# Zero products ahead of the first load, earlier routing loads and three copies on ScalarE in an attention and mixture-of-experts kernel

## The chip, the cores and the metric

The kernel runs on one core of a Trainium2 chip. The core has TensorE (matrix products, PE in the profile, with its weight loads as PEld), VectorE (DVE), ScalarE (ACT), GpSimd (POOL) and SyncE (SP), each with its own in-order queue of instructions; they meet at semaphores. DMA transfers are issued from such a queue (here mostly SP's). The metric is the device time of one execution in microseconds, as the median of several runs. A profile is one further execution that the hardware profiler took down.

## The reference

One sequence of S = 4096 rows with D = 256 columns, all in fp32, goes through one pre-norm block:

```python
x = x + attn(layernorm(x), Qw, Kw, Vw)          # causal, one head of 256
h = layernorm(x) @ W_in + b_in
logits = h @ W_gate + b_gate                    # 8 experts
topv, topi = top_k(softmax(logits), 2); topv /= sum(topv)
eout_e = relu(h @ W1[e] + b1[e]) @ W2[e] + b2[e]   # 256 -> 1024 -> 256
x = x + (sum over the two chosen e of topv * eout_e) @ W_out + b_out
```

## The kernel before, in words

The rows are held in SBUF in 8 blocks `xb[b]` of 512 rows (4 tiles of 128). The kernel has three stages.

*Attention, with the routing inside.* The weights of the queries and keys are folded into one: `prepare_scores` turns Qw and Kw with TensorE transposes into PSUM (L381, tiles pqwT and pkwT), ScalarE copies them out (L382), and TensorE multiplies them to pqk (L386), which VectorE scales into `qk_sb` (L393). For each block, `stats0` takes the layer norm's statistics on VectorE (L211, L212) with the reciprocal root on GpSimd (L217, L218); `ln_rows` makes the normalised rows z on VectorE (L231); `turn` transposes them (pz, L242) and VectorE copies them out as zT (L243); `project` makes the queries (pq, L406; copied as qT on VectorE, L413) and the values (pv, L418; copied on ScalarE, L425). `scores(g)` multiplies the scores of 256 queries with all keys up to them (ps, L448), adds the mask on the diagonal (L467), finds the row maxima (top, L473 to L478), turns them over with TensorE (pt, L484; pmax, L491), subtracts and takes the exponential (L495 to L504). `attend(g)` multiplies with the values (po, L513).

`prepare_biases` prepares the routing. It transposes a tile `brows`, which holds b1 (64 rows of 128) and b_in (2 rows), into pbias (L159); the copy biasT (L161) goes out to DRAM for the experts (L162). It transposes W_in, 128 columns at a time (pwin, L171), copies it out as winT (L172), multiplies it with W_gate (pwg, L176), and puts the product behind W_in's columns in `win_sb` (L183), so that one product later gives both h and the logits. b_in times W_gate (binc, L185; pbg, L190) is added to the gate's bias (L197). The transposes pbias and pwin take turns in two PSUM buffers (`ps_tr`), so the second half of pwin waits until biasT has been copied out of the first buffer.

*Experts.* Rows are scattered to the experts, taken in blocks of 256, halves and quarters; the weights of each come by DMA while TensorE works at the ones before (pm L743 and L773, pe L810). *The end.* The experts' results are read back, weighted, turned and multiplied with W_out (pa L997, pf L1011), added to x and stored.

What sets the order: each engine takes its instructions in the order of the built program. A scheduler decides that order from the order of the calls and from its own estimates, so instructions of `prepare_biases` stand among those of `scores(0)` and `scores(1)` on TensorE, and among the z of the second block on VectorE. `tc.issue_after` holds `stats0(1)` behind the projection of block 0. The loads at the front are issued from SP in the order of the calls (L119 to L136), with Kw and Qw ahead on ScalarE's queue (L107):

```python
for j in range(TPB):
    nc.sync.dma_start(out=xb[0][:, j, :], in_=xs[0][:, j, :])
vw_sb = load_square(Vw, "vw")
for b in range(1, NB):
    nc.sync.dma_start(out=xb[b], in_=xs[b])
```

After these come W_in, W_gate, W_out, the three bias rows and then brows.

Of the kernel before, what the change touches and what calls it, by code (L numbers as in the profile page):

```python
# [10 lines left out]
F32 = mybir.dt.float32  # L11
# [6 lines left out]
P = 128  # L18
# [3 lines left out]
QB = 256  # L22
# [12 lines left out]
def preln_attention_moe_kernel(  # L35
# [18 lines left out]
    nc = tc.nc  # L54

    _, S, D = x.shape
    NE, _, FF = W1.shape
    NT = S // P
    NB = S // TB
# [18 lines left out]
    xs = x.rearrange("o (b t p) d -> (o b) p t d", t=TPB, p=P)  # L78
    outs = out.rearrange("o (n p) d -> (o n) p d", p=P)

    const = ctx.enter_context(tc.tile_pool(name="const", bufs=1))
# [4 lines left out]
    def ps_mm(name):  # L86
        return psum.tile([P, TB], F32, tag="mm", name=name, bufs=4)

    def ps_tr(name):
        return psum.tile([P, TB], F32, tag="tr", name=name, bufs=2)  # L90

    def ps_o(name):
        return psum.tile([P, TB], F32, tag="o", name=name, bufs=2)
# [6 lines left out]
    parts = dram.tile([TOPK * S, D], F32, name="parts")  # L100


    xb = [stream.tile([P, TPB, D], F32, tag=f"x{b}", name=f"x{b}") for b in range(NB)]

    def load_square(w, name, queue=nc.sync):
        t = const.tile([P, ND, w.shape[1]], F32, tag=name, name=name)
        queue.dma_start(out=t, in_=w.rearrange("(c p) e -> p c e", p=P))  # L107
        return t

    def load_row(v, name):  # L110
        t = const.tile([P, v.shape[0]], F32, tag=name, name=name)
        nc.sync.dma_start(out=t, in_=v.partition_broadcast(P))
        return t
# [4 lines left out]
    for j in range(TPB):  # L118
        nc.sync.dma_start(out=xb[0][:, j, :], in_=xs[0][:, j, :])  # L119
    vw_sb = load_square(Vw, "vw")  # L120
    for b in range(1, NB):
        nc.sync.dma_start(out=xb[b], in_=xs[b])

    DG = D + NE
    win_sb = const.tile([P, ND, DG], F32, tag="win", name="win")
    nc.sync.dma_start(out=win_sb[:, :, :D], in_=W_in.rearrange("(c p) e -> p c e", p=P))
    wgate_sb = load_square(W_gate, "wgate")
    wout_sb = load_square(W_out, "wout")
    bgate_bc = load_row(b_gate, "bgate")
    bin_bc = load_row(b_in, "bin")  # L130
    bout_bc = load_row(b_out, "bout")

    NBR = NE * NF + ND
    brows = const.tile([NBR, P], F32, tag="brows", name="brows")
    nc.sync.dma_start(out=brows[: NE * NF, :], in_=b1.rearrange("e (f p) -> (e f) p", p=P))
    nc.sync.dma_start(out=brows[NE * NF :, :], in_=b_in.rearrange("(c p) -> c p", p=P))  # L136


    ident = const.tile([P, P], F32, tag="ident", name="ident")
# [5 lines left out]
        out=mask,  # L145
        in_=mask,
# [10 lines left out]
    def prepare_biases():  # L157
        ptb = ps_tr("pbias")
        nc.tensor.transpose(ptb[:, :NBR], brows, ident[:NBR, :NBR])  # L159
        biasT = const.tile([P, NBR], F32, tag="biasT", name="biasT")  # L160
        nc.vector.tensor_copy(biasT, ptb[:, :NBR])  # L161
        nc.sync.dma_start(  # L162
            out=bias1.rearrange("(e p) f -> p e f", p=P),
            in_=biasT[:, : NE * NF].rearrange("p (e f) -> p e f", f=NF),
        )

        winT = piece("winT", ND, D)
        for k in range(ND):
            pt = ps_tr(f"pwin{k}")
            for c in range(ND):  # L170
                nc.tensor.transpose(pt[:, ts(c, P)], win_sb[:, c, ts(k, P)], ident)  # L171
            nc.vector.tensor_copy(winT[:, k, :], pt[:, :D])  # L172
        for c in range(ND):
            pg = ps_o(f"pwg{c}")
            for k in range(ND):
                nc.tensor.matmul(  # L176
                    pg[:, :NE],
                    lhsT=winT[:, k, ts(c, P)],
                    rhs=wgate_sb[:, k, :],
                    start=(k == 0),  # L180
                    stop=(k == ND - 1),
                )
            nc.vector.tensor_copy(win_sb[:, c, D:], pg[:, :NE])  # L183
        binc = piece("binc", ND, P)
        nc.vector.tensor_copy(  # L185
            binc, biasT[:, NE * NF :].unsqueeze(2).to_broadcast([P, ND, P])
        )
        pg = ps_o("pbg")
        for k in range(ND):
            nc.tensor.matmul(  # L190
                pg[:, :NE],
                lhsT=binc[:, k, :],
                rhs=wgate_sb[:, k, :],
                start=(k == 0),
                stop=(k == ND - 1),
            )
        nc.vector.tensor_tensor(bgate_bc, pg[:, :NE], bgate_bc, ALU.add)  # L197
# [165 lines left out]
    def piece(name, *shape):  # L363

        return attn.tile([P, *shape], F32, tag="s", name=name, bufs=NS)
# [486 lines left out]
    for e in range(NE):  # L852
# [17 lines left out]
        out=rows[TOPK * (S - TB) :, :].rearrange("(t p) d -> p t d", p=P),  # L870
        in_=zero.unsqueeze(1).to_broadcast([P, TOPK * (TPB + 1), D]),
    )

    prepare_biases()
    row = scores(0)
    for g in range(NT // KU):
        b, q = divmod(g, QPB)
# [185 lines left out]
```

## Time and profile before

| What | Value |
|---|---|
| Median of 3 runs | 1119.69 us (1116.5 to 1120.69) |
| The profiled execution's own time | 1107.13 us |
| Its span | 1105.4 us |
| Granted TensorE clock, mean | 0.994 |
| TensorE busy | 1079.2 us |
| VectorE / ScalarE / GpSimd busy | 691.6 / 331.8 / 237.3 us |
| First product of TensorE | 5.61 us after the span's start |
| Front loads end | about 25 us after the span's start |

The table's busy times are sums over the whole span; what a single wait is worth is read from the chain of work that ended last and from the timelines, which give the start and duration of each instruction and, in brackets, how long its engine had been idle and what ended that. In the timelines one fp32 product appears as two records.

### The profile page before, as it was taken

How to read it: one execution, taken by the hardware profiler on the slowest of the kernel's cores; microseconds unless marked ns; L12 is line 12 of the kernel's file. 1: busy time of each engine (PE TensorE's matmuls, PEld its weight loads, DVE VectorE, ACT ScalarE, POOL GpSimd, SP SyncE). 2: the span in 40 equal slices, each digit the busy share in tenths (PEclk: the TensorE clock that was granted, in tenths of full speed). 3: DMA queues.
4: the chain of work that ended last, by engine and by line, in shares of the span. 5: the costliest groups of instructions: out<-in, count | busy, mean ns of one | idle time of the engine just before them, and what ended most of it. 6: DMA issues, size and time to landing. Idle time of an engine off the chain costs nothing.

```text
span 1105.4 us, 15667 instructions
## 1 busy us (share of the span) xinstructions
PE 1079.2 (98%) x5065; PEld 894.6 (81%) x5065; DVE 691.6 (63%) x2118; ACT 331.8 (30%) x727; POOL 237.3 (21%) x285
## 2 busy tenths in 40 slices
PE   7999999999999999999999999999999999999968
PEld 5778888888888888888888887777778686868857
DVE  4678575674664556445482844858587868678336
ACT  1323232332341423242222221232324232322334
POOL 2023211202102010201412422232323223231100
PEclk9999999999999999999999999999999999999979
DMA  8010101000001001001174575878888896977075
GB/s 264 1 38 1 39 1 39 1 19 21 1 1 39 1 1 39 1 1 39 52 243 160 146 244 169 295 256 273 278 288 294 276 325 217 338 221 257 25 287 180
DMA packets 114744, 148.34 MB, mean 134 GB/s; under 512 B 23005, under 2 KB 94626, under 8 KB 114660
## 3 DMA queue, kind: packets, MB, share of 16 engines
q1 hardware_dynamic: 105732, 129.70, 35.7%
q0 software_dynamic: 8384, 17.09, 4.6%
q8 instruction: 41, 0.67, 0.3%
q14 instruction: 43, 0.35, 0.2%
q10 hardware_dynamic: 544, 0.52, 0.1%
HBM read 124.79 MB, written 22.75 MB: 133 GB/s over the span
## 4 chain that ended last, share of the span: by engine, by line
PE 90%; DMA 5%; DVE 3%; issue 1%; POOL 0%; ACT 0%; SPq 0%; ACTq 0%; POOLq 0%; DVEq 0%
PE po L513 20%; PE ps L448 19%; PE pe_a L810 13%; PE pm_a L743 13%; DMA h_b<-rows,slot_b 4%; PE pf L1011 3%; PE ph L260 3%; PE pq L406 3%; PE pm_c L773 2%; PE pv L418 2%; PE pe_d L810 2%; PE pm_d L773 2%; PE pe_c L810 2%; PE pm_b L743 2%; PE pe_b L810 1%; PE pz L242 1%
## 5 line engine op out<-in xcount | busy, mean ns | idle before, releaser
L513 PE MATMUL po<-v,s 128*128 128x257 f32 x1056 | 238.3, 380 | 0.8 <-ACT s L504 0.7
L448 PE MATMUL ps<-qT,zT 128*128 128x256 f32 x1088 | 232.9, 374 | 0.0
L448 PEld LDWEIGHTS ps<-qT,zT 128*128 128x128 f32 x1088 | 202.9, 190 | 27.2 <-DVE mx L463 0.3
L513 PEld LDWEIGHTS po<-v,s 128*128 128x128 f32 x1056 | 197.0, 190 | 27.7 <-issue 1.6
L810 PE MATMUL pe_a<-w_a,mid_a 128*128 128x256 f32 x672 | 149.7, 380 | 0.0
L743 PE MATMUL pm_a<-hT_a,w_a 128*128 128x256 f32 x672 | 148.3, 379 | 0.0
L810 PEld LDWEIGHTS pe_a<-w_a,mid_a 128*128 128x128 f32 x672 | 127.0, 190 | 23.5 <-issue 6.7
L743 PEld LDWEIGHTS pm_a<-hT_a,w_a 128*128 128x128 f32 x672 | 127.7, 190 | 17.4
L752 ACT ACTIVATE mid_a<-pm_a,c_a 128x256 f32<-128x256 f32 x168 | 79.4, 473 | 196.7 <-PE pm_a L743 182.4
L457 ACT COPY s<-ps 128x512 f32<-128x512 f32 x120 | 70.3, 586 | 194.6 <-PE ps L448 154.9
L336 POOL DMA_INDIRECT slots<-assign,ati x64 | 62.7, 980 | 259.9 <-DVE ati L334 238.2
L463 DVE TENSOR_TENSOR mx<-ps,mx 128x512 f32<-128x512 f32 x91 | 62.8, 690 | 86.1 <-ACT s L457 85.5
L710 DVE STREAM_TRANSPOSE hT_a<-h_a 32x128 f32<-32x128 f32 x336 | 101.5, 302 | 4.5
L819 POOL DMA_INDIRECT parts<-y_a,slot_a x42 | 42.2, 1005 | 215.4 <-DVE y_a L818 197.4
L498 ACT ACTIVATE s<-s 128x512 f32<-128x512 f32 x120 | 71.7, 629 | 51.4 <-DVE s L495 50.9
L495 DVE TENSOR_TENSOR s<-s,pmax 128x512 f32<-128x512 f32 x120 | 73.1, 681 | 8.2 <-PE pmax L491 8.2
L818 DVE TENSOR_TENSOR y_a<-pe_a,c_a 128x256 f32<-128x256 f32 x42 | 16.7, 420 | 67.9 <-PE pe_a L810 56.5
L710 DVE STREAM_TRANSPOSE mid_c<-raw_c 32x256 f32<-32x256 f32 x128 | 55.8, 436 | 1.9
L639 POOL DMA_INDIRECT h_a<-rows,slot_a x42 | 41.0, 976 | 23.9 <-issue 10.5
L217 POOL TENSOR_SCALAR ln1rstd<-ln1mv 128x4 f32<-128x4 f32 x8 | 1.8, 228 | 202.5 <-DVE ln1mv L212 202.5
L710 DVE STREAM_TRANSPOSE mid_d<-raw_d 32x256 f32<-32x256 f32 x96 | 41.8, 436 | 1.5
L743 PE MATMUL pm_b<-hT_b,w_b 128*128 128x256 f32 x160 | 35.4, 379 | 0.0
(248 smaller groups left out, 1163.8 us busy)
## 6 DMA issues: line engine op xcount, KB each, us to landing
w_a<-in_L_ffn_W_dram SPq DMA_DIRECT2D x84, 512.0 KB, 6.6
w_d<-in_L_ffn_W_dram SPq DMA_DIRECT2D x48, 512.0 KB, 6.7
w_c<-in_L_ffn_W_dram SPq DMA_DIRECT2D x32, 512.0 KB, 7.3
w_b<-in_L_ffn_W_dram SPq DMA_DIRECT2D x20, 512.0 KB, 5.2
rows<-hr SPq DMA_DIRECT2D x16, 512.0 KB, 3.0
yp<-parts SPq DMA_DIRECT2D x14, 512.0 KB, 9.0
x<-in_L_attn_x_dram SPq DMA_DIRECT2D x7, 512.0 KB, 7.1
out_dram<-ot SPq DMA_DIRECT2D x14, 256.0 KB, 3.4
```

The source lines that it names most:

```text
L336: put = nc.gpsimd.indirect_dma_start(out=slots, out_offset=bass.IndirectOffsetOnAxis(ap=ati[:, j : j + 1], axis=0), in_=assign[:, b * TPB ...
L448: nc.tensor.matmul(ps[:, u * QB + lo : (u + 1) * QB], lhsT=zT[kt // TPB][:, d, ts(kt % TPB, P)], rhs=qT[b][:, d, q * QB + lo : (q + 1) * Q ...
L457: nc.scalar.copy(flat, ps)
L463: nc.vector.tensor_tensor(mx, ps, old, ALU.max)
L495: nc.vector.tensor_tensor(s, s, pm[:, :QB].unsqueeze(1).to_broadcast([P, KU, QB]), ALU.subtract)
L498: nc.scalar.activation(s, s, AF.Exp)
L513: nc.tensor.matmul(po[u][:, : D + 1], lhsT=ss[c][:, k, ts(u, P)], rhs=vb[kt // TPB][:, kt % TPB, :], start=(kt == 0), stop=(kt == g * KU + u),
L710: nc.vector.transpose(to[ts(f, SQ)][..., ts(q, SQ)], of[ts(q, SQ)][..., ts(f, SQ)])
L743: nc.tensor.matmul(pm[:, :SB], lhsT=w1[c][:, ts(f, P)], rhs=hT[:, c, :], start=(c == 0), stop=(c == ND - 1),)
L752: nc.scalar.activation(mid[f // 2][:, f % 2, :], pm[:, :SB], AF.Relu, bias=c1[:, f : f + 1])
L773: nc.tensor.matmul(pm[ts(j, rest), :], lhsT=hT[:, c, ts(j, rest)], rhs=w1[c][:, ts(i, TB)], start=(c == 0), stop=(c == ND - 1),)
L810: nc.tensor.matmul(pe[ts(j, rest), :D], lhsT=mid[f][:, ts(u, P)][:, ts(j, rest)], rhs=w2[f // (NF // 2)][:, f % (NF // 2), :], start=(f == 0),
```

## The change

Three edits, all of them at work in the first 30 us.

1. A tile of 128x128 zeros is set by VectorE, and TensorE multiplies it five times with itself (256 columns by a broadcast) into a PSUM buffer that nobody reads, ahead of its first product.
2. The loads of W_in, W_gate and both parts of brows are issued behind x's second block (`xb[1]`) instead of behind all eight, so ahead of the six blocks left.
3. The copies biasT (once) and winT (twice) run on ScalarE instead of VectorE.

```diff
+    zeros = const.tile([P, P], F32, tag="zeros", name="zeros")
+    nc.vector.memset(zeros, 0.0)
+    pw = ps_mm("warm")
+    for _ in range(5):
+        done = nc.tensor.matmul(
+            pw[:, :QB],
+            lhsT=zeros,
+            rhs=zeros.unsqueeze(1).to_broadcast([P, QB // P, P]),
+            start=True,
+            stop=True,
+        )
+        tc.keep_in_program_order(done)
...
     vw_sb = load_square(Vw, "vw")
-    for b in range(1, NB):
-        nc.sync.dma_start(out=xb[b], in_=xs[b])
+    nc.sync.dma_start(out=xb[1], in_=xs[1])
...
     nc.sync.dma_start(out=win_sb[:, :, :D], in_=W_in.rearrange("(c p) e -> p c e", p=P))
     wgate_sb = load_square(W_gate, "wgate")
+
+    NBR = NE * NF + ND
+    brows = const.tile([NBR, P], F32, tag="brows", name="brows")
+    nc.sync.dma_start(out=brows[: NE * NF, :], in_=b1.rearrange("e (f p) -> (e f) p", p=P))
+    nc.sync.dma_start(out=brows[NE * NF :, :], in_=b_in.rearrange("(c p) -> c p", p=P))
+    for b in range(2, NB):
+        nc.sync.dma_start(out=xb[b], in_=xs[b])
     wout_sb = load_square(W_out, "wout")
     bgate_bc = load_row(b_gate, "bgate")
     bin_bc = load_row(b_in, "bin")
     bout_bc = load_row(b_out, "bout")
-
-    NBR = NE * NF + ND
-    brows = const.tile([NBR, P], F32, tag="brows", name="brows")
-    nc.sync.dma_start(out=brows[: NE * NF, :], in_=b1.rearrange("e (f p) -> (e f) p", p=P))
-    nc.sync.dma_start(out=brows[NE * NF :, :], in_=b_in.rearrange("(c p) -> c p", p=P))
...
-        nc.vector.tensor_copy(biasT, ptb[:, :NBR])
+        nc.scalar.copy(biasT, ptb[:, :NBR])
...
-            nc.vector.tensor_copy(winT[:, k, :], pt[:, :D])
+            nc.scalar.copy(winT[:, k, :], pt[:, :D])
```

In the built program the products of zeros stand first on TensorE, the memset first on VectorE, and the three copies on ScalarE behind the last copy of v of block 0 and ahead of the first copy of s. On TensorE pwg's second half and pbg stand a few products earlier among those of ps, and on VectorE binc, the two copies into `win_sb` and the addition to the gate's bias stand around the first score operations in a slightly different order. From the transpose pt of the first group on, every engine's order is that of before.

## The prediction

> **What bounds the kernel now.** I read the page first (busy shares, then the chain of work that ended last), and after it the chain and the timelines of the first 35 us, since all the edits sit there. The page of the kernel before:
>
> ```profile
> span 1105.4 us, 15667 instructions
> PE 1079.2 (98%) x5065; PEld 894.6 (81%) x5065; DVE 691.6 (63%) x2118; ACT 331.8 (30%) x727; POOL 237.3 (21%) x285
> ...
> PE 90%; DMA 5%; DVE 3%; issue 1%; POOL 0%; ACT 0%; SPq 0%; ACTq 0%; POOLq 0%; DVEq 0%
> ```
>
> TensorE is busy for 1079.2 of 1105.4 us and carries 90% of the chain. A change pays only where it shortens TensorE's own work or one of its few waits; what is won at the front stays won if nothing later hangs on an absolute time. The chain of the first 80 us, in order of time (start, us, what):
>
> ```profile
> 1.22 4.25 DMA qw<-in_L_attn_Qw_dram
> ...
> 5.61 1.09 PE pqwT L381 x4
> 6.70 0.87 PE pkwT L381 x4
> 7.59 0.59 ACT kwT L382
> 8.22 3.78 PE pqk L386 x8
> 12.00 0.87 PE pz L242 x4
> 12.89 0.70 DVE zT L243
> 13.64 3.71 PE pq L406 x8
> ...
> 21.42 1.06 DVE z L231 x3
> 22.48 0.15 DVE biasT L161
> 22.67 0.44 PE pwin L171 x2
> ...
> 77.57 2.46 PE ps L448 x11
> ```
>
> TensorE first waits for Qw. Then pqk's 8 records of 128x256 take 3.78 us, 0.47 us each, while ps of the same shape later takes 2.46 for 11, 0.22 each: the front runs at half speed. The clock line of the page reads 9 there all the same, so the spacing of the products is the evidence, not that line. The second thing to see is VectorE's four z ahead of biasT, and TensorE waiting behind it. The timelines of VectorE, ScalarE and TensorE at those places (start, us, what, idle time before it and its releaser):
>
> ```profile
> 8.84 1.83 DVE L231 TENSOR_SCALAR z<-x,ln0rstd,ln0shift 128x256 f32<-128x256 f32 x4
> 10.59 0.41 DVE L393 TENSOR_SCALAR qk<-pqk 128x256 f32<-128x256 f32 x1
> 12.04 0.42 DVE L393 TENSOR_SCALAR qk<-pqk 128x256 f32<-128x256 f32 x1 [1.04 <-PE pqk L386]
> 12.89 1.29 DVE L243 COPY zT<-pz 128x512 f32<-128x512 f32 x2 [0.43 <-PE pz L242]
> ...
> 22.40 0.22 DVE L161 COPY biasT<-pbias 128x66 f32<-128x66 f32 x1
> ```
>
> ```profile
> 20.83 0.37 ACT L425 COPY v<-pv 128x256 f32<-128x256 f32 x1 [0.49 <-PE pv L418]
> 24.97 0.27 ACT L471 COPY s<-ps 128x128 f32<-128x128 f32 x1 [3.77 <-DVE s L467]
> ```
>
> ```profile
> 20.63 0.22 PE L159 MATMUL pbias<-ident,brows 66*128 66x66 f32 x1
> 22.67 0.44 PE L171 MATMUL pwin<-ident,win 128*128 128x128 f32 x2 [1.16 <-DVE biasT L161]
> ```
>
> [...]from pqk's start at 8.22 to the first product at full spacing, about 11.8, is 3.6 us. Near the end TensorE is almost idle from 1054 to 1063, the clock view then reads 0.50, and full speed is back near 1070. Idle stretches of 1.0 to 1.5 us at 21.5, 29.5 and 32.8 did not cost the clock. [...]the trace shows 339 to 380 GB/s from 3 to 15 us, so the front loads fill the transfers, and order among them decides when each lands.
>
> **The change, part by part.**
>
> *Five products of zeros.* Added: one VectorE memset of 128x128 and 5 fp32 products of 128x256, 10 records. POOL's memset of that size takes 0.20 us. Other engines' first instructions stand at 0.26 to 1.74, so I take the products to start at 0.9; bounds 0.5 and 2.0. At half speed a record is spaced 0.43 (pqk), so 10 take 4.3 and end at 5.2, under TensorE's 5.6 us wait for Qw: no cost. By 3.6 us of sustained work the clock is released at 4.5, and the last records go faster. Even starting at 2.0 they end at 6.3 at the latest, 0.7 us into pqwT, which is later covered by slack (below). VectorE's memset is covered by its wait for x, until 3.68.
>
> At full clock pqwT (4 transposes spaced 0.11 instead of 0.21) ends at 6.2 instead of 6.7; ScalarE copies qwT until 6.8 and kwT until 7.45; pqk starts at 7.5 and takes 8 x 0.213 + 0.15 = 1.85, ending at 9.35 instead of 12.0. The full 2.65 us isn't gained, for VectorE is next: its order z, qk, qk, zT stays. The four z end at 10.6, held by the statistics and POOL's power, which the edit doesn't touch. The first qk stays at 10.59, the second moves from 12.04 to 10.98, zT from 12.89 to 11.37, pz being ready by about 11.0. So pq starts **1.5 us** earlier. Slack under it: pqk's end at 9.35 may slip 1.2 us, which covers the late start. If the clock isn't released, 0; it can't exceed 1.5 unless this profile's release was an early one[...].
>
> *Loads.* Win, wgate and both brows loads are issued behind x1 instead of x7, on SP's queue, four issues past six x loads. In the order of the build nothing else of SP moves; wout, the bias rows, slots and the zero rows stay behind x. The gain by itself is nil: pbias had no wait for brows at 20.63. But brows' second part is issued at 17.92 and x was still landing; with TensorE coming 1.5 us sooner, at 19.1, it would have been late by up to 1.5. The move is cover for the first part, and I keep that as its price if it failed. Now about 2.1 MB lie up to brows, 6 us at 350 GB/s, so it lands by 12 at the latest, 7 us of slack. What is late instead: x2 by 0.3 MB, about 1 us, and its statistics run near 52. bgate has as many bytes ahead as before plus brows' 33 KB (0.1 us), lands near 19.7 (issue 13.56 + 6.0) and is wanted after 22. Cost 0.
>
> *Copies on ScalarE.* VectorE loses 0.22 + 2 x 0.41 = 1.04 us, ScalarE gains about 0.2 + 2 x 0.37 = 0.95. In the order of the build the three stand on ScalarE right behind the last v copy and ahead of s L471, where it idled 3.77 us: free. They no longer queue behind z. With the 1.5 us: v ends at 19.7, biasT at 19.9, so pwin's second turn, which waits for biasT, starts at 20.0 instead of 22.67; winT's first half ends at 20.3 and pwg starts at 20.33 instead of 23.05: 2.7 us in all, **1.2 us** from this part. From there to pt TensorE has the same records, in a slightly other order (pwg and pbg go ahead of some of ps), 3.6 us: pt at 23.9 instead of 26.64. The waits inside: winT's second half (20.8, wanted 21.2), binc on VectorE behind z (21.65, pbg at 22.0), top (23.3, pt at 23.9). Each has 0.3 us or more to spare. Bounds of this part: 0.6, if binc or biasT come later than that, and 1.5. Where the stall goes: at 29.65 and 31.03 TensorE waits for exp and top as before, VectorE's chain there being relative.
>
> *Sum.* 1.5 + 0 + 1.2 = 2.7 us. Behind pt the order on all engines is the one of before, and every wait (attention, the expert stage, the 9 us round trip near 1053) is relative to work in front of it. The profiled execution goes from 1107.13 to 1104.4 (span 1105.4 to 1102.7). The timed median, 1119.69, stands 12.56 above the profiled execution, and I carry that over: **1117.0**.
>
> **Rivals.**
> - *The clock isn't released by the products* (zeros may count less[...]). pqk stays at 3.78, only ScalarE's part works: 1.2, so 1118.5. For it: the release at 11.8 came only after an unbroken stretch. Against: 4.3 us of products are longer than the 3.6 us that sufficed.
> - *More is won*: [...]Then pz and pq also ran slowly[...]: 4.4, 1115.3.
> - *It is absorbed*: a later stage starts on something fixed, and the gain ends there: 1119.7. Against: after 25 us the transfers read 0 to 11 GB/s per slice until the first rows go out, and no DMA of the chain is tied to the front.
> - *Slower*: the granted clock in the dense stretch (60 to 1053) falls. It was 0.994; the timed runs are 1.1% above the profile, so something of this size exists. Each 0.1% costs 1.1 us; from 0.25% on the gain is gone, and 0.8% gives 1125.9. Against: the change adds 4 us of products to 1079.
>
> **How the numbers follow.** Forecast 0.62, no release 0.12, more 0.12, absorbed 0.08, slower 0.06. What a measurement of this kernel can tell from no change is about 0.5%, 5.6 us: faster lies below 1114.1, slower above 1125.3. The three runs of before spread by 4.2 us, so a median may shift by 2. The 2.7 us are half the bound; faster takes half of "more" and a fifth to a quarter of the forecast's scatter: 0.20; slower 0.05; same 0.75. The range reaches from 4.4 won and 2.5 of scatter, 1112.8, to 1.2 won and 2.0 of scatter, 1120.5.
>
> **What would show it.** Right: five products between about 0.9 and 5.3; pqk's 8 records in about 1.9; the second qk right behind the first near 11; pq near 12.1; biasT, winT on ScalarE near 19.7 to 20.8; no wait of pwin for biasT over 0.3; pt near 23.9; ps of later groups earlier by 2.7 throughout. Wrong: pqk still at 3.8; TensorE waiting for brows or win; a shift that shrinks between 24 us and 1053 us, or a granted clock below 0.99.

## The result and the profile after

Over 18 runs each, the changed kernel takes 1116.24 us in the median (1113.91 to 1118.38), the kernel before 1118.41 (1116.27 to 1120.69). The ratio is 0.9979, with a 95% interval of 0.9970 to 0.9988: 1.3 to 3.4 us won, 2.3 in the middle, where 2.7 had been forecast. The gain is clear of zero and below the 0.5% that the prediction set as its bound.

The page of the changed kernel (all its line numbers behind the zeros are 15 higher than before):

```profile
span 1112.1 us, 15687 instructions
PE 1083.2 (97%) x5075; PEld 896.1 (81%) x5075; DVE 691.4 (62%) x2116; ACT 332.2 (30%) x730; POOL 236.9 (21%) x285
```

Here is the first trap of this case: the profiled span is 6.7 us *longer* than that of before (1105.4), while the timed runs are shorter. A good part of that is a wait of 5.8 us in the expert stage, which a second profile of the kernel before shows as well (below). So spans of the two aren't compared below, but times at the same place of the front. The timeline of TensorE in the changed kernel (start, us, what, idle time before it and its releaser):

```profile
1.06 4.22 PE L107 MATMUL warm<-zeros 128*128 128x256 f32 x10 [1.06 <-DVE zeros L104]
5.43 0.63 PE L396 MATMUL pqwT<-ident,qw 128*128 128x128 f32 x4
...
7.22 1.99 PE L401 MATMUL pqk<-kwT,qwT 128*128 128x256 f32 x8 [0.73 <-ACT kwT L397]
...
12.12 3.70 PE L421 MATMUL pq<-zT,qk 128*128 128x512 f32 x8 [0.49 <-DVE zT L258]
...
19.11 0.22 PE L174 MATMUL pbias<-ident,brows 66*128 66x66 f32 x1
...
19.86 0.44 PE L186 MATMUL pwin<-ident,win 128*128 128x128 f32 x2
...
23.75 0.27 PE L499 MATMUL pt<-ident,top 128*128 128x128 f32 x1
```

pqk takes 1.99 us instead of 3.78, pq starts at 12.12 instead of 13.64, pwin's second half has lost its wait for biasT, and the first pt stands at 23.75 instead of 26.64, 2.89 us earlier. The timelines of VectorE and ScalarE show what is the bound now:

```profile
8.98 1.83 DVE L246 TENSOR_SCALAR z<-x,ln0rstd,ln0shift 128x256 f32<-128x256 f32 x4
10.73 0.73 DVE L408 TENSOR_SCALAR qk<-pqk 128x256 f32<-128x256 f32 x2
11.39 1.27 DVE L258 COPY zT<-pz 128x512 f32<-128x512 f32 x2
```

```profile
19.58 0.22 ACT L176 COPY biasT<-pbias 128x66 f32<-128x66 f32 x1
19.69 0.39 ACT L187 COPY winT<-pwin 128x256 f32<-128x256 f32 x1
```

z, the two qk and zT follow each other on VectorE without a gap: the wait for pqk (1.04 us) is gone, and x's statistics set the start of pq. On ScalarE the copies come right behind the last v.

### The profile page after: what moved, and what is told of

The parts are those of the page before. It is cut to its first block, busy times and chain, and to the rows that moved or that the text cites. A ratio compares the mean times of both kernels' runs of the same rounds, so it can differ in the third digit from the quotient of the medians.

```text
span 1112.1 us, 15687 instructions
## 1 busy us (share of the span) xinstructions
PE 1083.2 (97%) x5075; PEld 896.1 (81%) x5075; DVE 691.4 (62%) x2116; ACT 332.2 (30%) x730; POOL 236.9 (21%) x285
## 4 chain that ended last, share of the span: by engine, by line
PE 81%; issue 6%; DMA 5%; DVE 3%; POOL 2%; another core or an unknown queue 1%; SPq 0%; ACT 0%; POOLq 0%; ACTq 0%; DVEq 0%
PE po L528 19%; PE ps L463 19%; PE pm_a L758 12%; PE pe_a L825 11%; DMA h_b<-rows,slot_b 4%; PE ph L275 3%; PE pf L1026 3%; PE pq L421 3%; PE pv L433 2%; PE pm_c L788 2%; PE pm_d L788 2%; PE pe_c L825 2%; PE pe_d L825 1%; PE pz L257 1%
## 5 line engine op out<-in xcount | busy, mean ns | idle before, releaser
L758 PE MATMUL pm_a<-hT_a,w_a 128*128 128x256 f32 x672 | 151.1, 384 | 5.8 <-ACT mid_a L767 5.8
```

Source lines behind the costliest of these rows:

```text
L758: nc.tensor.matmul(pm[:, :SB], lhsT=w1[c][:, ts(f, P)], rhs=hT[:, c, :], start=(c == 0), stop=(c == ND - 1),)
```

## The experiments

The measure for the front is the start of the first pt, since every order behind it is that of before. One profile doesn't settle it alone: two profiles of the kernel before have the first pt at 26.64 and 26.03. So the table splits it for all kernels into three stretches that add up to it: until VectorE starts the first z (set by when x lands), from z to pq (where the products of zeros act), and from pq to pt (where the copies and brows act). All times are in us, read from the timelines.

| Kernel | z starts | z to pq | pq to pt | pbias waits for brows | first pt |
|---|---|---|---|---|---|
| Before | 8.84 | 4.80 | 13.00 | none | 26.64 |
| Before, second profile | 8.86 | 3.94 | 13.23 | 1.39 | 26.03 |
| Zeros alone | 10.08 | 3.14 | 13.38 | 1.53 | 26.60 |
| Copies alone | 8.85 | 4.08 | 12.35 | 0.59 | 25.28 |
| After | 8.98 | 3.14 | 11.63 | none | 23.75 |
| After, second profile | 8.81 | 3.14 | 11.63 | none | 23.58 |
| After, loads in the old order | 8.84 | 3.14 | 13.06 | 1.30 | 25.04 |
| After, copies on VectorE | 8.71 | 3.14 | 13.00 | none | 24.85 |
| After, two products | 11.07 | 3.14 | 11.63 | none | 25.84 |
| After, ten products | 10.08 | 3.14 | 11.63 | none | 24.85 |

Three things stand in it. In three executions x's last piece landed 1.1 to 2.3 us late, and pt with it, whatever the edit. With five products or more z to pq takes 3.14, without any 3.94 to 4.80, so five are worth 0.8 to 1.7 (the 3.14 with two products has another reason, told there). And pq to pt falls to 11.63 only where the copies are on ScalarE *and* the loads are early; either without the other leaves 12.35 to 13.06. The moved loads alone, and the change without any products, were not run.

### Each edit alone

*Zeros alone.* On the kernel before:

```diff
+    zeros = const.tile([P, P], F32, tag="zeros", name="zeros")
+    nc.vector.memset(zeros, 0.0)
+    ...                       # the five products, as in the change
```

> The kernel before plus the zeros and their five products alone. The measure is the start of the first turning product pt: 26.64 us before, 23.75 after. My sum: pq starts near 12.1 instead of 13.64, but biasT and winT stay on VectorE behind z, so the first pt is at 25.1 to 25.2 (1.5 won); pbias may wait for brows without moving biasT. Rival, that the products alone carry the whole gain: 23.8. Rival, that the clock is released by something else: 26.6.

The first pt came at 26.60: nothing won of the 1.5 forecast. The timelines of TensorE and of VectorE in that kernel:

```profile
13.22 3.70 PE L420 MATMUL pq<-zT,qk 128*128 128x512 f32 x8 [0.49 <-DVE zT L257]
21.91 0.25 PE L173 MATMUL pbias<-ident,brows 66*128 66x66 f32 x1 [1.53 <-DMA brows<-in_L_ffn_b_dram]
```

```profile
7.66 0.43 DVE L225 BATCH_NORM_STATS2 bn<-x 128x6 f32<-128x256 f32 x1 [1.08 <-DMA x<-in_L_attn_x_dram]
...
10.08 1.83 DVE L245 TENSOR_SCALAR z<-x,ln0rstd,ln0shift 128x256 f32<-128x256 f32 x4
```

pqk took 1.99 us, so the products do release the clock by themselves, and z to pq is 1.66 shorter. But two loads were late in this execution. x's last piece came late, so z started 1.24 later than before. And pbias waited 1.53 us for brows, which lengthens pq to pt by only 0.38: biasT, still on VectorE, had to wait for three z anyway. Together these undo the 1.66. brows' second part was issued at 19.47 here and at 17.92 in the first profile of before, because SP was busy for 9.13 us instead of 7.50 with the seven loads of x ahead. Both my number and the rival that the products carry the gain fell; what the products alone win when x is on time wasn't measured.

*Copies alone.* On the kernel before:

```diff
-        nc.vector.tensor_copy(biasT, ptb[:, :NBR])
+        nc.scalar.copy(biasT, ptb[:, :NBR])
-            nc.vector.tensor_copy(winT[:, k, :], pt[:, :D])
+            nc.scalar.copy(winT[:, k, :], pt[:, :D])
```

> The kernel before with biasT and winT copied by ScalarE alone. My sum: pqk stays at 3.8 us, pwin's second half starts near 21.5 instead of 22.67, the first pt at 25.4 (1.2 won). Rival, that the copies only work once TensorE is early: 26.3 or later.

The first pt came at 25.28 (25.4 expected), pwin's second half at 21.48 (21.5). The agreement is luck: 0.72 of the 1.36 won comes from z to pq, the clock having come sooner than in the first profile (pqk 3.46 us, not 3.78), and only 0.65 from the copies, as pbias waited 0.59 us for brows.

### Each edit taken out of the change

*The loads in the old order.* The kernel after with this undone:

```diff
-    nc.sync.dma_start(out=xb[1], in_=xs[1])
+    for b in range(1, NB):
+        nc.sync.dma_start(out=xb[b], in_=xs[b])
     ...                       # W_in, W_gate, W_out, bias rows, brows behind
```

> The kernel after with all loads in the old order: the zeros and the copies without the moved loads. My theory, that the moved loads are cover for the other two: pbias, which could start at 19.1, waits for brows until between 19.5 and 20.6, and the first pt comes at 24.1 to 25.2. Rival, that the move of the loads does nothing even here: no wait ahead of pbias and pt at 23.75.

```profile
20.43 0.25 PE L173 MATMUL pbias<-ident,brows 66*128 66x66 f32 x1 [1.30 <-DMA brows<-in_L_ffn_b_dram]
```

TensorE came to pbias at 19.1 and waited 1.30 us for brows; the first pt stood at 25.04, 1.29 later than in the kernel after. The theory that the moved loads are cover holds, with the wait that the prediction named. What they cover is above all the copies: with brows this late, pq to pt takes 13.06, as long as with the copies on VectorE.

*The copies back on VectorE*, in the kernel after (the second diff above, reversed):

> The kernel after with biasT and winT copied by VectorE again: zeros and moved loads without the copies. My sum puts 1.2 us on the copies: biasT stands behind z at about 20.9, pwin's second half waits about 1.2 us for it and the first pt comes at 24.9 to 25.1. Rival, that with the loads early the copies are worth nothing: 23.75.

```profile
20.88 0.44 PE L186 MATMUL pwin<-ident,win 128*128 128x128 f32 x2 [1.16 <-DVE biasT L176]
```

The wait of before is back, 1.16 us, and the first pt stands at 24.85, 1.10 later than in the kernel after, though z started 0.27 sooner. From pq to pt the copies are worth 1.37 where the loads are early, about what the sum said. Early loads without the copies leave pq to pt at 13.00, as before.

*Two products instead of five*, in the kernel after:

```diff
-    for _ in range(5):
+    for _ in range(2):
```

> The kernel after with two products of zeros instead of five. My theory, sustained work of about 3.6 us is wanted: 1.7 us of products end near 2.8, TensorE then idles 2.6 us, the clock is not released before pqk, which takes 3 to 3.8 us; pq starts at 13.0 to 13.6 and the first pt comes at 24.7 to 25.4. Rival, any first work sets the release going: pqk in 2.0, pt at 23.75.

```profile
1.06 2.07 PE L107 MATMUL warm<-zeros 128*128 128x256 f32 x4 [1.06 <-DVE zeros L104]
...
8.21 3.78 PE L401 MATMUL pqk<-kwT,qwT 128*128 128x256 f32 x8 [0.67 <-ACT kwT L397]
```

```profile
8.65 0.43 DVE L226 BATCH_NORM_STATS2 bn<-x 128x6 f32<-128x256 f32 x1 [2.08 <-DMA x<-in_L_attn_x_dram]
...
11.07 1.83 DVE L246 TENSOR_SCALAR z<-x,ln0rstd,ln0shift 128x256 f32<-128x256 f32 x4
12.82 0.74 DVE L408 TENSOR_SCALAR qk<-pqk 128x256 f32<-128x256 f32 x2
```

The products end at 3.1, TensorE idles 2.46 us, and pqk is as slow as before. So it isn't any first work that releases the clock; whether the smaller amount or the gap is what counts isn't separated here. pt came at 25.84, 2.09 later than with five, but that is not the price of the slow pqk: x's last piece landed late, z started 2.09 later, and pqk, done at 11.99, was ahead of the end of z. What two products cost when x is on time wasn't measured.

*Ten products instead of five* (the same line with 10):

> The kernel after with ten products of zeros instead of five. My theory, the clock is released near 4.7 to 5.3 and the later records are spaced 0.21: the products end near 7.4, 2 us into the time of pqwT, the slack ahead of zT takes 1.2 to 1.6 of it, pq starts at 12.4 to 12.6 and the first pt comes 0.3 to 0.5 later than in the kernel after, at 24.1 to 24.3. Rival, there is no slack: pt 2 us later, 25.8. Rival, the clock stays at half speed until the first real product: the products end at 9.5 and pt comes at 26 or later.

The products ended at 7.43 as expected, pqwT began there, and pqk took 1.99 us. pt came at 24.85, 1.10 later. But in this execution x's last piece landed late: VectorE waited for it and started the last statistics at 7.67 instead of 6.56, and z started at 10.08 instead of 8.98, 1.10 later. The whole delay is thus x's, and the products' overrun of 2.0 us cost nothing that can be seen. How much slack there is when x is on time wasn't measured.

### The same two kernels once more

Nothing is edited in these two; they were run side by side on one chip.

> The kernel before as it is, for a second profile: its first one, at 1107.13 us, is 9 us under the fastest of its 18 timed runs (1116.27). If the difference of the two first profiles in the expert stage (a wait of 5.8 us of TensorE for ScalarE's mid_a near 632 us, in the profile after alone) comes from run to run, a wait of 4 to 9 us stands in this profile in the same place and the time is near 1118. If it comes from the change, this profile has no wait of TensorE above 0.5 us between 590 and 1050. The first pt at 26.6 in either case.

> The kernel after as it is, for a second profile. The first pt at 23.7 to 23.9 and pqk in 2.0 us if the five products release the clock in each run[...]. The wait near 632 us: 4 to 9 us if it belongs to most runs of both kernels.

The waits of TensorE, first in the second profile of the kernel before, then in the first of the kernel after (us in total, times, longest):

```profile
PE pm_a L743 <- ACT mid_a L752: 6.5, 1, 6.5
```

```profile
PE pm_a L758 <- ACT mid_a L767: 5.8, 1, 5.8
```

The kernel before has the wait as well, at 1115.89 us, so it doesn't come from the change. Over all profiles: the first one of before and the four that ran together on one chip at 1104.5 to 1106.3 us show none; the other nine, the second of before and eight of kernels built on the change, show 4.3 to 6.6 us near 632 to 640. One of the four without it, the kernel with two products, has all the moved loads and copies, so neither kernel is tied to either side. In the kernel after, ScalarE there stands still for 16 us and goes on at 637.26, in front of an instruction that reads the expert's biases c_a, whose load was issued at 619.68. That this load came late is an inference from those two times; why it does on some chips stays open.

In the front, the second profile of before had its first pt at 26.03 instead of the 26.6 expected (the clock came sooner, pqk took 3.44 and pq started at 12.80; pbias waited 1.39 us for brows), the second of after at 23.58. There the five products took 4.63 us, pqwT still ran slowly (1.08 us), and the clock came during the next transposes; pqk took 1.99 all the same. So the gain at pt is 2.3 to 3.1 us by which profiles are paired.

Does it last? From the first pt to the start of the expert stage (587.52 in the kernel before) TensorE's order is the same in all fourteen profiles. In the five profiles without the wait this stretch took 560.9 to 561.0 us, in the kernel before as with the edits: there what was won at pt lasts to about 0.1. In the other nine it took 563.2 in the second profile of before and 563.3 to 564.9 in the kernels built on the change. So of the 2.45 at pt between the two second profiles 0.83 is left at the expert stage (589.24 to 588.41), and with ten products nothing (589.74). But those eight profiles still differ by 1.6 us among themselves, as much as is missing, so one pair doesn't show an absorption. The timed gain, 1.3 to 3.4 us, admits both.

### Going on from the change

*x ahead of Qw and Kw*, on the kernel after:

```diff
-    kw_sb = load_square(Kw, "kw", nc.scalar)
-    qw_sb = load_square(Qw, "qw", nc.scalar)
     for j in range(TPB):
-        nc.sync.dma_start(out=xb[0][:, j, :], in_=xs[0][:, j, :])
+        queue = nc.scalar if j % 2 else nc.sync
+        queue.dma_start(out=xb[0][:, j, :], in_=xs[0][:, j, :])
+    kw_sb = load_square(Kw, "kw", nc.sync)
+    qw_sb = load_square(Qw, "qw", nc.scalar)
...
-            nc.vector.tensor_scalar_mul(qk_sb[:, c, :], pp[:, :D], QSCALE)
+            nc.scalar.mul(qk_sb[:, c, :], pp[:, :D], QSCALE)
```

> The kernel after, with the four pieces of x's first block issued ahead of Kw and Qw, two on each queue, and qk scaled by ScalarE instead of VectorE. My theory, after the change the chain to pq runs over x, the statistics, z and zT, and pqk has slack: z starts near 7.5 instead of 8.98, zT near 9.8, pq at 10.4 to 10.8 instead of 12.12, and the whole is 1.3 to 1.7 us faster than the kernel after. Rival, TensorE's own chain from Qw is as late: pq stays within 0.4 of 12.12.

z did start earlier, at 7.26 instead of 8.98, and yet pq came at 13.45 and pt at 25.05. The timeline of TensorE:

```profile
1.06 4.39 PE L107 MATMUL warm<-zeros 128*128 128x256 f32 x10 [1.06 <-DVE zeros L104]
6.68 0.63 PE L397 MATMUL pqwT<-ident,qw 128*128 128x128 f32 x4 [1.23 <-DMA qw<-in_L_attn_Qw_dram]
...
8.47 3.67 PE L402 MATMUL pqk<-kwT,qwT 128*128 128x256 f32 x8 [0.73 <-ACT kwT L398]
```

Qw landed 1.2 us later, and the clock was lost: pqwT is still fast (0.63), pqk slow. The spacing of pqk's records is 0.43 us (10.76, 11.19, 11.62), as in the kernel before (10.09, 10.52), and not 0.21 to 0.22 as in the kernel after (7.76, 7.97, 8.19). Of the two gaps the kernel after has the 0.73 ahead of pqk as well, but not the 1.23. The ratio to the kernel before was 0.9989 (0.9980 to 0.9998), so the 1.3 to 1.7 us beyond the change did not come; whether some of the change's own gain was lost the overlapping intervals don't tell.

*Zeros at the end*, on the kernel after: 17 more products of zeros between the last expert product and the first gathered rows.

```diff
+    pw = ps_mm("warm2")
+    for _ in range(17):
+        ...                   # the same product and order as at the front
     HT = TPB // 2
```

> The kernel after, with 17 more products of zeros on TensorE ahead of the first gathered rows at the end, in the idle stretch in which the experts' results go out and come back (9 us, after which the clock view reads 0.50). My theory: at full clock 17 products take 7.3 us, the clock is kept, the first 8 records of pf take 1.9 instead of 3.6, and the whole is 2.0 to 2.6 us faster than the kernel after. Rival, the end is bound by the transfers and ScalarE's weighting: less than 0.7 us.

```profile
1071.25 1.99 PE L1037 MATMUL pf<-wout,aT 128*128 128x256 f32 x8 [0.62 <-ACT aT L1028]
```

The first eight records of pf take 1.99 us; they took 3.59 in the kernel after. The ratio to before is 0.9966 (0.9954 to 0.9978), the best of all; against the change's own 0.9979 that is 1.5 us in the middle, measured at another time and with overlapping intervals, so faster than before is shown and faster than the change is only likely. And the profiles don't show that the fast pf is the cause. The last expert products and a later stretch of pf, in the kernel after and then with zeros at the end:

```profile
1048.40 13.98 PE L825 MATMUL pe_b<-w_b,mid_b 128*128 128x256 f32 x64
...
1077.99 2.76 PE L1026 MATMUL pf<-wout,aT 128*128 128x256 f32 x12
```

```profile
1045.77 13.98 PE L825 MATMUL pe_b<-w_b,mid_b 128*128 128x256 f32 x64
...
1074.75 0.83 PE L1023 MATMUL pa<-ident,acc 128*128 128x128 f32 x4 [0.63 <-DVE acc L1014]
1075.42 2.75 PE L1037 MATMUL pf<-wout,aT 128*128 128x256 f32 x12
```

From the end of the expert products to the twelve records of pf it is 15.61 us in the one and 15.67 in the other: behind the fast pf TensorE waits for the weighted rows (acc). The 2.6 us by which this profile is ahead lie before the zeros at the end. The rival, that the end is bound by the transfers and the weighting, is not excluded.

*Both together*:

> The edits of the two kernels before this one together, on the kernel after. Additive by my theory: 3.3 to 4.3 us faster than the kernel after, 5.5 to 7 us faster than the kernel before, a ratio to it of 0.994 to 0.995. If one end's gain is absorbed on the way: 0.996 to 0.9975.

0.9983 (0.9975 to 0.9991): not additive. In the profile Qw landed at 7.80, 2.38 us behind the products, pqk took 3.78, pq started at 15.36 and pt at 26.96. At the end, too, pf took 3.37 us, so the zeros there don't keep the clock each time. The profiled execution, 1117.05 us, is one of the longer of its 21 runs (1110.76 to 1117.72), so it needn't stand for all.

*Both, with eight products at the front* instead of five:

> The kernel with both ends' edits, with eight products of zeros at the front instead of five. With x's pieces ahead, Qw landed 1.2 to 2.4 us after the five products had ended, pqwT still ran fast (0.63 us) and pqk slow (3.7 us). My theory, the idle gap took the clock back: eight products end near 6.7, pqk takes 2.0 us, and pq starts at 11.2 to 12.3 by when Qw lands, instead of 13.45 and 15.36; the whole is 1.5 to 2.5 us faster than the kernel after. Rival, the clock does not follow the gap: pqk stays above 3.4 us.

```profile
1.06 6.06 PE L107 MATMUL warm<-zeros 128*128 128x256 f32 x16 [1.06 <-DVE zeros L104]
...
8.91 1.99 PE L402 MATMUL pqk<-kwT,qwT 128*128 128x256 f32 x8 [0.72 <-ACT kwT L398]
```

With the gap filled up to Qw, pqk takes 1.99 us again. So the clock was lost in both kernels with the gap and kept in this one without it: with one profile of each, this supports the theory that the gap had taken the clock. But pq starts at 12.21 and pt at 23.81, as in the kernel after, because Qw, pushed back, is as late as x was: the rival named for x ahead of Qw and Kw holds. The whole is 0.9992 (0.9984 to 1.0001) of before, against my expectation; at the end pf took 3.29 us. With pt where the change has it, it should have been as fast as the change; its interval only touches the change's (0.9970 to 0.9988), and what takes the rest on that chip stays open.

## Why the prediction was right, and where it was off

- *The forecast as a whole* (1117.0, 2.7 us won, within 0.5%): measured 1116.24 and 2.3 us won, inside the range and of the forecast's sign and size. The 1117.0 was counted from a median of three runs, 1.3 above that of 18, so the difference is the better test of the two.
- *Products of zeros.* Start 1.06 (0.9 forecast), end 5.28 (5.2), pq at 12.12 (near 12.1), 1.5 won there: right to 0.1 us, and so was the choice to let VectorE's chain, not pqk's 1.8 us, set the gain. The gain itself is 0.8 to 1.7 from z to pq, by which profile of before it is held against.
- *The release of the clock.* That the products release it in time was right, but the number behind it was misread, and that it held was luck and slack. The prediction read 3.6 us of work up to full speed from the profile of before, taking pz, from 11.8 on, to run at full spacing. It did not: four of pz's transposes take 0.87 us (the chain's line at 12.00), as long as pkwT's at half speed, and the spacing falls from 0.21 to 0.11 near 12.9. So the trace says 4.7 us from the start of pqk, more than the 4.2 that the products last. In the kernel after the spacing of the products falls at the last of the ten records, near 4.8; in its second profile only near 7, during the transposes of Kw (pkwT 0.93 us, 1.06 in the kernel before). It didn't matter, as pqk (done at 10.08 there) had slack ahead of VectorE's second qk. The moment differs between profiles of one kernel (pqk of before: 3.78 and 3.44 us); the prediction used one value. That it is the length of the work that counts was my estimate from that one reading: behind five, eight and ten products (4.2 to 6.5 us) pqk took 1.99 us where work followed within 0.4 us; behind two (2.07 us) it took 3.78, but there TensorE idled 2.46 us ahead of Qw as well.
- *Loads.* "Up to 1.5 us of cover" measured 1.30. What I misjudged is the starting point: from one profile I took pbias to have no wait for brows. The second profile has one of 1.39 us; in the first TensorE came just after brows, which landed 2.4 to 2.6 us behind its issue where a wait shows it, so at about 20.4 there (an estimate from the issue at 17.92). With the copies on VectorE waits of 1.39 and 1.53 cost only 0.23 and 0.38 from pq to pt, hidden behind z; with the copies on ScalarE one of 1.30 cost 1.43. The prediction had the loads as cover for the products; the runs show them as the other half of the copies.
- *Copies.* 1.2 forecast, 1.37 from pq to pt measured by taking them out, 0.65 by adding them alone with brows late.
- *Sum at pt.* 23.9 forecast, 23.75 and 23.58 measured.
- *Carrying 12.56 us from profile to median.* The gap was not explained then. The nine profiles at 1109.5 us of span and above have a wait of 4 to 7 us in the expert stage which that one did not have, and 2 to 4 us more between pt and the expert stage. The forecast was spared by being a difference.
- *Rivals.* No release: excluded at the front of the kernel after, in both profiles. Absorption: excluded as a whole by the interval, open for about 1 us on some chips. More won because the clock of before comes later in other runs: the size given for it was my estimate, which no trace had shown, and it was not seen; in the two further profiles without products it came sooner (pqk 3.44 and 3.46). A lower clock in the dense stretch: the granted clock was 0.992 in the profile after and 0.991 in both second profiles, on one chip, so no difference there.
- *A claim of the prediction that fell:* that idle stretches of 1.0 to 1.5 us did not cost the clock. At the three places that it names the timeline of before has 1.16, 0.67 and 0.96 us, between dense products, and there it holds; with x ahead of Qw, 1.23 and 0.73 us with only transposes between them went with a lost clock.

## What to carry to other kernels

Edits at the front that shorten one engine's start pay only as far as the next arrival allows, so work out for each what lands next and move that too: here the copies were worth 1.37 us with the loads early and nothing with brows 1.3 us late, and the early loads nothing without the copies. Filling TensorE's idle start with useless work cost nothing here, as x arrived later than pqk was ready (pqk ended at 9.21, the last z at 10.81); two products did not release the clock (pqk 3.78 us), and gaps of 1.23 and 2.38 us behind five went with its loss. And one profile is one execution: before a difference is put down to a change, take a second profile of the kernel before, and look whether the loads at the head of the chain landed at the same time; late pieces of x moved pt here by as much as the change did.

## What the runs showed of the hardware that was not expected

- Five products at half speed (4.2 to 4.6 us) had the clock at full speed by pqk (1.99 us) in each of the six profiles in which real work followed within 0.4 us; the moment of release differed by about 2 us. After 1.23 us and 2.38 us of further idleness pqwT still ran fast (0.63 us) and pqk, two us later, at half speed (3.67 and 3.78). At the end, with transposes scattered over 2.8 to 5.0 us between the zeros and pf, the clock was kept once (pf 1.99) and lost twice (3.37, 3.29), and not by the length of that stretch: it was kept over 3.6 and lost over 2.8.
- The clock view reads 1.00 over the first 12 us of the kernel before, in which pqk runs at half speed (3.78 us), but 0.50 from 1058 to 1070, where the first eight records of pf take 3.78 us.
- With the old load order pbias started at 20.63 without a wait, and at 20.67, 20.43, 21.34 and 21.91 after waits for brows of 0.59, 1.30, 1.39 and 1.53 us. The scatter of 1.5 us is that of the issue: brows landed 2.4 to 2.6 us behind it in all four, and SP came to it later where the loads of x ahead took longer.
- x's last piece of the first block let VectorE start its last statistics at 6.3 to 6.6 in eight profiles with x behind Qw, and at 7.66, 7.67 and 8.65 in three.
- Chips differ: on one the kernel before took 1105.42 us in a single run, and four kernels near to it 1104.5 to 1106.3; on two others it took 1116.74 and 1116.62 in the median, on a fourth 1120.09 and 1115.89 in single runs. The wait of 4 to 7 us near 635 is part of the difference.
